# Layer 0 of a two-layer block: each part of the features written to DRAM once and repeated by the loads, sums of the weights taken from SBUF, reciprocals stored once

## The chip, the cores and the metric

The kernel runs on one core of a Trainium2 chip. The metric is the device time of one execution in microseconds; before the change its median is 2718.08 us of three runs (2716.01 to 2725.01).

The core's engines run side by side, each through its own instructions in order: TensorE (PE in the profile, with its weight loads as PEld), VectorE (DVE), ScalarE (ACT), GpSimd (POOL) and SyncE (SP), which here does nothing but issue DMAs. Sixteen DMA engines move the data. SBUF is the on-chip memory of 128 partitions, PSUM the accumulators that TensorE writes.

## The reference

Two layers of gated cross-attention and mixture-of-experts work on 64 sequences of 128 positions and 128 channels; 77 context rows belong to each sequence. The change concerns the attention of layer 0 alone:

```python
def _feature_map(x, fm_w, fm_b):
    z = jnp.einsum('nshd,ed->nshe', x, fm_w) + fm_b
    return jnp.concatenate([jnp.exp(z), jnp.exp(-z)], axis=-1)
...
v, k, q = (_feature_map(x, fm_w, fm_b) for x in (v, k, q))
scores = jnp.einsum('nqhd,nkhd->nhqk', q, k) / jnp.sqrt(jnp.float32(EMBED))
attn = jax.nn.softmax(scores, axis=-1)
out = jnp.einsum('nhql,nlhd->nqhd', attn, v)
out = out.reshape(N, S, HEADS * EXP_DIM)
return out @ fc_w.T + fc_b
```

There are 16 heads of 8 channels; the features of a head are 16, the eight exponentials of z and the eight of -z. Queries come from the normalized x, keys and values from the context. After it come layer 0's experts (eight, of width 336, with a learned number of them for each row), layer 1's attention with relative positions, and layer 1's experts (eight of width 256, the best two).

## The kernel before

**Units.** Layer 0 works on 32 units of two sequences (`NU = 2`, so 256 query columns `UT` and 154 context columns `UK`). The loop in `run` (L1086) goes through them as a pipeline: in step k it weaves together `l0_project` of unit k-3, `l0_weighted` of k-2, `l0_maxima` of k-1, `l0_features` of k, in every other step `l0_route`, and a "tape" of pieces of the experts of earlier groups. `PLAN` gives each stream a stretch of the step and a priority; the instructions are then laid out for each engine by a planner that works with its own estimates of durations. What each engine runs is fixed by that order.

**Features** (`l0_features`, L290). x and the context are loaded (L296, L298), normalized, transposed (L304, L306) and multiplied by a block matrix (L311) into the PSUM tile `pz`: rows are (feature, head), 128 of them, columns are the 256 query and the 154 context positions. ACT takes the exponential of z and of -z, queries and context apart (L315, L316), into the tile `f` (called `feat` in the profile). TensorE transposes the context's part for the values (L327).

Scores are wanted in nearly full precision from bfloat16 products. So `split3` (L132) cuts the features into three bfloat16 parts that add up to them, in the tile `f3`, 128 partitions by 3 parts by 820 columns: DVE copies part 0 (L135), POOL subtracts it (L136), DVE copies part 1 (L137), POOL subtracts again into part 2 (L138). A product is then the sum of six pairs of parts. The six pairs lie on the contraction axis: `qst` has 96 partitions, six times 16 features, of 16 heads by 256 columns, with query parts 0,0,0,1,1,2; `kst` the same of 16 heads by 154 columns, with key parts 0,1,2,0,1,0. In `f3` the partitions are (feature, head), in `qst` and `kst` they are (pair, feature) with the heads along the row, so the data go through DRAM: `stack_out` (L140) writes the arrays `dq` and `dk` with each part as often as it is needed (six stores), and four loads (L340, L342) bring them back, those of the features of z to partitions 0 to 47 and those of -z to 48 to 95. A row of a load is one head's 256 or 154 columns, 512 or 308 bytes. All these DMAs go out on SP.

**Scores.** `l0_maxima` (L346) multiplies `qst[:96]` and `kst[:96]` (L355) for the largest score of each row and head; its negative, split in three, is loaded into `qst`'s partitions 96 to 98 (L371) beside rows of ones in `kst`. `l0_weighted` (L373) multiplies again with all 99 partitions (L396), so that the maximum is taken off within the product, takes the exponential (L399) and multiplies by the values (L385). The values have a column of ones, so the product's row 16 of each group of 32 partitions is the sum of the weights. ACT copies the result to the tile `av` (L388): 128 partitions (four groups j of 32 rows), 4 heads, 2 sequences, 128 queries.

**Normalization** (`normalize`, L428, called from L409). `av` is stored to the DRAM array `od` (L408). From there `den`, the sums, is loaded to 32 partitions (L435), and `o`, the 16 feature rows of each head, to 128 (L439, two loads). DVE takes the reciprocal (L440); it is stored 16 times over to `dr` (L442), loaded as `rr` in the layout of `o` (L445), and POOL multiplies (L446). `l0_project` (L411) multiplies `o` by the output weights (L420).

Of the kernel before, what the change touches and what calls it, by code (L numbers as in the profile page):

```python
# [10 lines left out]
F32 = mybir.dt.float32  # L11
F32R = mybir.dt.float32r
BF16 = mybir.dt.bfloat16
AF = mybir.ActivationFunctionType
# [6 lines left out]
KL = 77  # L21
NH = 16
# [6 lines left out]
NU = 2  # L29
UT = NU * S  # L30
UK = NU * KL
# [10 lines left out]
def weave(tc, streams, marks=None):  # L42
# [30 lines left out]
    out=(0,0.2,2000,0),  # L73
# [31 lines left out]
class Net:  # L105
# [26 lines left out]
    def split3(self, f, out3):  # L132
# [3 lines left out]
        nc.gpsimd.tensor_tensor(f, f, out3[:, 0], ALU.subtract)  # L136
        nc.vector.tensor_copy(out3[:, 1], f)  # L137
        nc.gpsimd.tensor_tensor(out3[:, 2], f, out3[:, 1], ALU.subtract)  # L138

    def stack_out(self, dq, dk, f3, nq):  # L140

        nc = self.nc
        for n, c, p in ((0, 3, 0), (3, 2, 1), (5, 1, 2)):
            nc.sync.dma_start(out=dq[n : n + c].rearrange("i p t -> p i t"),
                              in_=f3[:, p, :nq].unsqueeze(1).to_broadcast([128, c, nq]))
            nc.sync.dma_start(out=dk[n : n + c].rearrange("i p t -> p i t"), in_=f3[:, :c, nq:])

    def stack_q(self, dq, f3, nq):
        for n, c, p in ((0, 3, 0), (3, 2, 1), (5, 1, 2)):
# [140 lines left out]
    def l0_features(self, u, st):  # L290
        nc, i, tc = self.nc, self.i, self.tc
        a, pm, dp = self.ap, self.pmisc, self.dp
        b0 = u * NU
        kst, (vf, va) = self.kst[u % 3], self.va[u % 3]
        xg = self.f0.tile([128, NU, 128], F32, tag="xg", bufs=4, name="xg")
        nc.sync.dma_start(out=xg, in_=i["x"][b0 : b0 + NU].rearrange("b p d -> p b d"))  # L296
        cg = a.tile([KL, NU, 128], F32, tag="cg", bufs=2, name="cg")
        nc.sync.dma_start(out=cg, in_=i["ctx_1024"][b0 : b0 + NU].rearrange("b p d -> p b d"))  # L298
        xn = self.layernorm(xg, NU, a, "a")
        nc.gpsimd.tensor_tensor(xg, xg, self.fcb.unsqueeze(1).to_broadcast([128, NU, 128]), ALU.add)  # L300
        NT = UT + UK
        pt = pm.tile([128, 512], F32, tag="misc", name="pt")
        for b in range(NU):
            nc.tensor.transpose(pt[:, b * S : (b + 1) * S], xn[:, b, :], self.ident)  # L304
        for b in range(NU):
            nc.tensor.transpose(pt[:, UT + b * KL : UT + (b + 1) * KL], cg[:, b, :], self.ident[:KL, :KL])  # L306
        xT = a.tile([128, NT], F32, tag="xT", bufs=1, name="xT")
        nc.scalar.copy(xT, pt[:, :NT])
        yield
        pz = pm.tile([128, 512], F32, tag="misc", name="pz")  # L310
        nc.tensor.matmul(pz[:, :NT], lhsT=self.fmW, rhs=xT, start=True, stop=True)  # L311

        f = a.tile([128, 2 * NT], F32, tag="feat", bufs=1, name="feat")
        for n, sign in ((0, 1.0), (1, -1.0)):
            nc.scalar.activation(f[:, n * UT : (n + 1) * UT], pz[:, :UT], AF.Exp, bias=self.fmb[:, n : n + 1], scale=sign)  # L315
            nc.scalar.activation(f[:, 2 * UT + n * UK : 2 * UT + (n + 1) * UK], pz[:, UT:NT], AF.Exp,  # L316
                                 bias=self.fmb[:, n : n + 1], scale=sign)
        yield
        if u < 3:
            with tc.issue_after(self.ln_last.ins):  # L320
                nc.vector.memset(kst[96:99], 1.0)
            nc.gpsimd.memset(va[:, :, :, 16:17], 1.0)

        for b in range(NU):
            pv = pm.tile([128, 512], F32, tag="misc", name="pv")
            for s in range(2):
                nc.tensor.transpose(pv[:KL, s * 128 : (s + 1) * 128],  # L327
                                    f[:, 2 * UT + s * UK + b * KL : 2 * UT + s * UK + (b + 1) * KL], self.ident)
            nc.scalar.copy(va[:, b, :, 0:16],
                                  pv[:KL, :256].rearrange("p (c h) -> p h c", h=NH))  # L330
        f3 = a.tile([128, 3, 2 * NT], BF16, tag="f3", bufs=1, name="f3")
        yield
        self.split3(f, f3)
        yield
        dq = dp.tile([6, 128, 2 * UT], BF16, tag="dq", name="dq")
        dk = dp.tile([6, 128, 2 * UK], BF16, tag="dk", name="dk")
        self.stack_out(dq, dk, f3, 2 * UT)
        qst = a.tile([99, NH, UT], BF16, tag="qst", bufs=3, name="qst")
        for n in range(2):
            nc.sync.dma_start(out=qst[48 * n : 48 * n + 48],  # L340
                              in_=dq[:, :, n * UT : (n + 1) * UT].rearrange("i (e h) t -> (i e) h t", h=NH))
            self.last_dma = nc.sync.dma_start(out=kst[48 * n : 48 * n + 48],  # L342
                              in_=dk[:, :, n * UK : (n + 1) * UK].rearrange("i (e h) t -> (i e) h t", h=NH))
        st[u] = dict(xg=xg, qst=qst, kst=kst, va=vf, spare=[Spare(self.pGU, self.gub)] * 4 if u < 2 else [])

    def l0_maxima(self, s):  # L346
# [26 lines left out]
    def l0_weighted(self, s):  # L373

        nc, a = self.nc, self.ap
        ps_t, qst, kst, va = self.pST, s["qst"], s["kst"], s["va"]
        av = a.tile([128, 4, NU, 128], F32, tag="av", bufs=1, name="av")
# [13 lines left out]
        for b in range(NU):  # L391
            for hg in range(4):
                st = next(banks).tile([128, 4, 128], F32, tag="ST", name="ST")
                for j in range(4):
                    h = 4 * j + hg
                    nc.tensor.matmul(st[:KL, j, :], lhsT=kst[:, h, b * KL : (b + 1) * KL],  # L396
                                     rhs=qst[:, h, b * S : (b + 1) * S], start=True, stop=True)
                p = a.tile([KL, 4, 128], F32, tag="P", bufs=3, name="P")
# [7 lines left out]
        T = NU * S  # L406
        od = self.dp.tile([4, 32, 4, T], F32, tag="od16", name="od")
        nc.sync.dma_start(out=od.rearrange("j r g t -> (j r) g t"), in_=av.rearrange("p g b q -> p g (b q)"))  # L408
        s["o"] = self.normalize(od, 16, NU)  # L409

    def l0_project(self, u, s, x1s):  # L411
        nc, pm = self.nc, self.pmisc
# [12 lines left out]
            x1s[u // 2] = self.x1n  # L425
        yield

    def normalize(self, od, nd, n):  # L428


        nc, a, dp = self.nc, self.ap, self.dp
        nch = nd * NH // 128
        T = n * S
        den = a.tile([NH * n, 128], F32, tag="den", bufs=1, name="den")
        nc.sync.dma_start(out=den, in_=od[:, nd].rearrange("j g (b q) -> j (g b) q", b=n))  # L435
        o = self.f0.tile([128, nch, T], F32, tag="o", bufs=2, name="o")
        ny = 4 // nch
        for y in range(ny):
            nc.sync.dma_start(out=o[y::ny], in_=od[:, :nd, y * nch : (y + 1) * nch].rearrange("j d c t -> d j (c t)"))  # L439
        nc.vector.reciprocal(den, den)  # L440
        dr = dp.tile([nd, NH * n, 128], F32, tag=f"dr{nd}_{n}", name="dr")
        nc.sync.dma_start(out=dr.rearrange("d p q -> p d q"),  # L442
                          in_=den.unsqueeze(1).to_broadcast([NH * n, nd, 128]))
        rr = a.tile([128, nch, T], F32, tag="rr", bufs=1, name="rr")
        nc.sync.dma_start(out=rr, in_=dr.rearrange("d (x c b) q -> (d x) c (b q)", c=nch, b=n))  # L445
        nc.gpsimd.tensor_tensor(o, o, rr, ALU.mult)  # L446
        return o

# [814 lines left out]
```

## Time and profile before

The profile is one execution taken by the hardware profiler.

| | |
|---|---|
| time of the profiled execution | 2721.63 us |
| its span, first to last instruction | 2719.9 us |
| mean granted TensorE clock | 0.94 |
| PE busy | 2409.3 us (89%) |
| DVE busy | 1996.1 us (73%) |
| ACT busy | 1563.2 us (57%) |
| POOL busy | 1551.5 us (57%) |
| DMA packets, data | 468652, 282.16 MB, 104 GB/s |
| L342 `kst` loads | 64, first issue 25.3 us, last 1263.4 us |
| stretch 420 to 1260 us: PE busy | 770.96 us of 840 |

In the profile "L355" is line 355 of the kernel; "out<-in" are the tiles written and read. A wait belongs to the instruction that waited and names what ended it. "The chain" is the work that ended last, followed back from the end: at each step to what released it, or to the instruction before it on its engine. The granted clock is the share of its full speed at which TensorE was let run. Layer 0 covers about the first half of the span, layer 1 the second. In the list of transfers, `dq<-f` and `dk<-f` are the six stores, `qst<-dq` and `kst<-dk` the loads.

### The profile page before, as it was taken

How to read it: one execution, taken by the hardware profiler on the slowest of the kernel's cores; microseconds unless marked ns; L12 is line 12 of the kernel's file. 1: busy time of each engine (PE TensorE's matmuls, PEld its weight loads, DVE VectorE, ACT ScalarE, POOL GpSimd, SP SyncE). 2: the span in 40 equal slices, each digit the busy share in tenths (PEclk: the TensorE clock that was granted, in tenths of full speed). 3: DMA queues.
4: the chain of work that ended last, by engine and by line, in shares of the span. 5: the costliest groups of instructions: out<-in, count | busy, mean ns of one | idle time of the engine just before them, and what ended most of it. 6: DMA issues, size and time to landing. Idle time of an engine off the chain costs nothing.

```text
span 2719.9 us, 60927 instructions
## 1 busy us (share of the span) xinstructions
PE 2409.3 (89%) x23574; PEld 1655.9 (61%) x23574; DVE 1996.1 (73%) x4165; ACT 1563.2 (57%) x3030; POOL 1551.5 (57%) x1508
## 2 busy tenths in 40 slices
PE   3688989999989899999897798998999998999996
PEld 2466666666666666666565565666666666666654
DVE  3368788888888888887785466776677676766676
ACT  2455555656555556555454356666666666666665
POOL 4455465555565555554566355665666666656556
PEclk9989899999999999999997689999999999999999
DMA  6744355354454443453235655545555655655400
GB/s 140 172 107 93 78 114 117 93 107 104 83 122 106 94 111 91 100 120 73 57 80 130 137 115 112 119 110 107 107 112 109 121 127 116 126 111 109 95 16 8
DMA packets 468652, 282.16 MB, mean 104 GB/s; under 512 B 231030, under 2 KB 446974, under 8 KB 468267
## 3 DMA queue, kind: packets, MB, share of 16 engines
q1 hardware_dynamic: 440715, 237.89, 43.4%
q10 hardware_dynamic: 27648, 40.38, 4.3%
q8 instruction: 185, 3.03, 0.5%
q14 instruction: 104, 0.85, 0.1%
HBM read 143.00 MB, written 134.40 MB: 102 GB/s over the span
## 4 chain that ended last, share of the span: by engine, by line
PE 49%; DMA 16%; DVE 13%; POOL 9%; issue 7%; ACT 3%; SPq 3%; POOLq 0%; ACTq 0%; DVEq 0%
DMA kst<-dk 5%; PE ST L837 4%; PE py L165 3%; PE py L166 3%; PE py L167 3%; PE AV L845 3%; DMA dk<-f 2%; PE AV L385 2%; POOL hl L1001 2%; PE S L780 2%; PE pu L165 2%; PE pg L165 2%; PE pz L165 2%; PE S L885 2%; POOL f L138 2%
## 5 line engine op out<-in xcount | busy, mean ns | idle before, releaser
L524 POOL TENSOR_TENSOR hl<-t,hh 128x512 fp32r<-128x512 f32 x336 | 441.8, 1317 | 352.3 <-ACT hh L523 348.2
L1001 POOL TENSOR_TENSOR hl<-t,hh 128x512 fp32r<-128x512 f32 x256 | 347.0, 1371 | 148.0 <-ACT hh L1000 145.3
L829 POOL TENSOR_TENSOR sc<-sc,mx 128x308 f32<-128x308 f32 x256 | 190.3, 747 | 229.4 <-DVE mx L828 94.8
L523 ACT CAST hh<-t 128x512 fp32r<-128x512 f32 x336 | 207.2, 617 | 162.5 <-PE py L167 68.8
L516 ACT ACTIVATE t<-pg 128x512 f32<-128x512 f32 x336 | 200.9, 598 | 158.3 <-PE pg L167 114.2
L517 DVE SCALAR_TENSOR_TENSOR t<-t,pg 128x512 f32<-128x512 f32 x336 | 227.7, 678 | 74.6 <-ACT t L516 74.0
L838 ACT ACTIVATE rel<-ST 77x512 f32<-77x512 f32 x256 | 157.7, 616 | 170.4 <-PE ST L837 166.7
L518 DVE TENSOR_TENSOR t<-t,pu 128x512 f32<-128x512 f32 x336 | 227.3, 677 | 15.1 <-PE pu L167 6.7
L623 DVE TENSOR_TENSOR ys<-sb,py 128x512 f32<-128x512 f32 x224 | 152.0, 679 | 79.2 <-PE py L167 78.3
L827 DVE TENSOR_TENSOR sc<-S,rq 128x308 f32<-128x308 f32 x256 | 120.2, 472 | 120.6 <-PE ST L837 50.3
L614 ACT COPY sb<-pb 128x512 f32<-128x512 f32 x256 | 150.5, 588 | 97.4 <-PE pb L609 94.2
L837 PE MATMUL ST<-ident,sc 128*128 128x128 f32 (+1 forms) x1024 | 173.9, 296 | 35.1 <-POOL sc L829 33.0
L1000 ACT CAST hh<-t 128x512 fp32r<-128x512 f32 x256 | 155.5, 622 | 83.6 <-PE py L167 75.0
L993 ACT ACTIVATE t<-pz 128x512 f32<-128x512 f32 x256 | 151.9, 600 | 69.9 <-POOL hl L1001 64.1
L399 ACT ACTIVATE P<-ST 77x512 f32<-77x512 f32 x256 | 151.0, 591 | 57.9 <-PE ST L396 55.1
L165 PE MATMUL py<-hh,wd_h 128*128 128x512 f32 x336 | 156.9, 467 | 18.5 <-ACT sb L614 11.9
L165 PE MATMUL pg<-xh,wg_h 128*128 128x512 f32 x336 | 159.9, 476 | 11.5 <-DVE t L518 10.5
L358 DVE TENSOR_REDUCE mx<-S 128x5 f32<-128x385 f32 (+1 forms) x192 | 110.4, 577 | 78.2 <-PE S L355 76.6
L837 PEld LDWEIGHTS ST<-ident,sc 128*128 128x128 f32 (+1 forms) x1024 | 126.4, 152 | 66.6 <-POOL sc L829 42.0
L165 PE MATMUL pu<-xh,wu_h 128*128 128x512 f32 x336 | 159.9, 476 | 5.0 <-DVE t L517 4.5
L166 PE MATMUL py<-hl,wd_h 128*128 128x512 f32 x336 | 148.6, 442 | 2.3 <-POOL hl L524 2.3
L995 DVE TENSOR_TENSOR t<-t 128x512 f32<-128x512 f32 x128 | 106.6, 833 | 50.9 <-ACT t L993 50.8
(247 smaller groups left out, 6627.4 us busy)
## 6 DMA issues: line engine op xcount, KB each, us to landing
rq<-ra SPq DMA_DIRECT2D x256, 154.0 KB
qst<-dq SPq DMA_DIRECT2D x96, 384.0 KB
ra<-sg ACTq DMA_DIRECT2D x128, 192.5 KB
kst<-dk SPq DMA_DIRECT2D x96, 231.0 KB
dq<-f SPq DMA_DIRECT2D x47, 384.0 KB
od<-av SPq DMA_DIRECT2D x32, 512.0 KB
ra<-sg ACTq DMA_DIRECT2D x64, 231.0 KB
dq<-f SPq DMA_DIRECT2D x47, 256.0 KB
```

The source lines that it names most:

```text
L165: nc.tensor.matmul(ps, lhsT=wh, rhs=xh, start=start, stop=False)
L166: nc.tensor.matmul(ps, lhsT=wh, rhs=xl, start=False, stop=False)
L516: nc.scalar.activation(t, pg, AF.Tanh, scale=0.5)
L517: nc.vector.scalar_tensor_tensor(t, t, 1.0, pg, ALU.add, ALU.mult)
L518: nc.vector.tensor_tensor(t, t, pu, ALU.mult)
L523: nc.scalar.copy(hh, t)
L524: nc.gpsimd.tensor_tensor(hl, t, hh.bitcast(F32), ALU.subtract)
L829: nc.gpsimd.tensor_tensor(sc, sc, m.unsqueeze(2).to_broadcast([128, 4, KL]), ALU.subtract)
L837: nc.tensor.transpose(st[:r, j, :], sc.rearrange("q j k -> q (j k)")[:, j * KL : j * KL + r], self.ident)
L838: nc.scalar.activation(relg[:KL, hg, b], st[:KL].rearrange("k j (q e) -> k j q e", e=2), AF.Exp, scale=1.0 / math.sqrt(HD))
L1000: nc.scalar.copy(hh, t)
L1001: nc.gpsimd.tensor_tensor(hl, t, hh.bitcast(F32), ALU.subtract)
```

## The change

Five things change, all in layer 0:

1. The exponentials write `f` with query and context columns side by side for each sign, so one ACT instruction of 410 columns takes the place of two (L315, L316). `f` now has the order (sign, query columns, context columns).
2. `stack_out` is gone. Each part is stored once, queries and context together: parts 0 and 1 to `d01`, part 2 to `d2`, two stores on SP.
3. Six loads take the place of four. A load that needs a part or a pair of parts several times has a source whose outermost dimension repeats it (`to_broadcast`): `qst` partitions 0 to 47 are part 0 three times, `kst` 16 to 79 are parts 0 and 1 twice, `qst` 48 to 79 are part 1 twice; `kst` 80 to 95 are part 0, `qst` 80 to 95 and `kst` 0 to 15 are part 2. The pairs are then in another order (query parts 0,0,0,1,1,2 against key parts 2,0,1,0,1,0), and all 16 features of a pair lie together. The loads that need part 0 and 1 alone come first.
4. `den` is loaded straight from `av` in SBUF, not from `od`.
5. `dr` holds each reciprocal once; the load of `rr` repeats it 16 times.

```diff
-    def stack_out(self, dq, dk, f3, nq):
-        nc = self.nc
-        for n, c, p in ((0, 3, 0), (3, 2, 1), (5, 1, 2)):
-            nc.sync.dma_start(out=dq[n : n + c].rearrange("i p t -> p i t"),
-                              in_=f3[:, p, :nq].unsqueeze(1).to_broadcast([128, c, nq]))
-            nc.sync.dma_start(out=dk[n : n + c].rearrange("i p t -> p i t"), in_=f3[:, :c, nq:])
...
         for n, sign in ((0, 1.0), (1, -1.0)):
-            nc.scalar.activation(f[:, n * UT : (n + 1) * UT], pz[:, :UT], AF.Exp, bias=self.fmb[:, n : n + 1], scale=sign)
-            nc.scalar.activation(f[:, 2 * UT + n * UK : 2 * UT + (n + 1) * UK], pz[:, UT:NT], AF.Exp,
-                                 bias=self.fmb[:, n : n + 1], scale=sign)
+            nc.scalar.activation(f[:, n * NT : (n + 1) * NT], pz[:, :NT], AF.Exp, bias=self.fmb[:, n : n + 1], scale=sign)
...
-        dq = dp.tile([6, 128, 2 * UT], BF16, tag="dq", name="dq")
-        dk = dp.tile([6, 128, 2 * UK], BF16, tag="dk", name="dk")
-        self.stack_out(dq, dk, f3, 2 * UT)
+        d01 = dp.tile([2, 256, NT], BF16, tag="d01", name="d01")
+        d2 = dp.tile([1, 256, NT], BF16, tag="d2", name="d2")
+        for d, p0, p1 in ((d01, 0, 2), (d2, 2, 3)):
+            nc.sync.dma_start(out=d.rearrange("i (n p) t -> p (i n) t", n=2),
+                              in_=f3[:, p0:p1].rearrange("p i (n t) -> p (i n) t", n=2))
         qst = a.tile([99, NH, UT], BF16, tag="qst", bufs=3, name="qst")
-        for n in range(2):
-            nc.sync.dma_start(out=qst[48 * n : 48 * n + 48],
-                              in_=dq[:, :, n * UT : (n + 1) * UT].rearrange("i (e h) t -> (i e) h t", h=NH))
-            self.last_dma = nc.sync.dma_start(out=kst[48 * n : 48 * n + 48],
-                              in_=dk[:, :, n * UK : (n + 1) * UK].rearrange("i (e h) t -> (i e) h t", h=NH))
+        q, k = slice(0, UT), slice(UT, NT)
+        for to, row, n, src in ((qst, 0, 3, d01[:1, :, q]), (kst, 16, 2, d01[:, :, k]), (qst, 48, 2, d01[1:, :, q]),
+                                (kst, 80, 1, d01[:1, :, k]), (qst, 80, 1, d2[:, :, q]), (kst, 0, 1, d2[:, :, k])):
+            src = src.rearrange("i p t -> (i p) t")
+            rows = n * src.shape[0] // 16
+            if n > 1:
+                src = src.unsqueeze(0).to_broadcast([n, *src.shape])
+            self.last_dma = nc.sync.dma_start(out=to[row : row + rows], in_=src)
...
-        s["o"] = self.normalize(od, 16, NU)
+        s["o"] = self.normalize(av, od, 16, NU)
...
-        nc.sync.dma_start(out=den, in_=od[:, nd].rearrange("j g (b q) -> j (g b) q", b=n))
+        nc.sync.dma_start(out=den, in_=av[nd::32].rearrange("j g b q -> j (g b) q"))
...
-        dr = dp.tile([nd, NH * n, 128], F32, tag=f"dr{nd}_{n}", name="dr")
-        nc.sync.dma_start(out=dr.rearrange("d p q -> p d q"),
-                          in_=den.unsqueeze(1).to_broadcast([NH * n, nd, 128]))
+        dr = dp.tile([NH * n, 128], F32, tag=f"dr{nd}_{n}", name="dr")
+        nc.sync.dma_start(out=dr, in_=den)
         rr = a.tile([128, nch, T], F32, tag="rr", bufs=1, name="rr")
-        nc.sync.dma_start(out=rr, in_=dr.rearrange("d (x c b) q -> (d x) c (b q)", c=nch, b=n))
+        nc.sync.dma_start(out=rr, in_=dr.rearrange("p q -> (p q)").unsqueeze(0).to_broadcast([nd, NH * n * 128]))
```

More of the change, by code (lines that the diff above doesn't have):

```diff
@@ L327, in l0_features @@
                 nc.tensor.transpose(pv[:KL, s * 128 : (s + 1) * 128],
-                                    f[:, 2 * UT + s * UK + b * KL : 2 * UT + s * UK + (b + 1) * KL], self.ident)
+                                    f[:, s * NT + UT + b * KL : s * NT + UT + (b + 1) * KL], self.ident)
             nc.scalar.copy(va[:, b, :, 0:16],
@@ L426, in l0_project, with normalize @@
         yield
-    def normalize(self, od, nd, n):
+    def normalize(self, av, od, nd, n):
         nc, a, dp = self.nc, self.ap, self.dp
```

## The prediction

> **What bounds the kernel now.** I read the page's chain first, then the chain piece by piece in the middle of layer 0, then the waits, then the DMA view in short windows. The page's chain, by engine and by line:
>
> ```profile
> PE 49%; DMA 16%; DVE 13%; POOL 9%; issue 7%; ACT 3%; SPq 3%; POOLq 0%; ACTq 0%; DVEq 0%
> DMA kst<-dk 5%; PE ST L837 4%; PE py L165 3%; PE py L166 3%; PE py L167 3%; PE AV L845 3%; DMA dk<-f 2%; PE AV L385 2%; POOL hl L1001 2%; PE S L780 2%; PE pu L165 2%; PE pg L165 2%; PE pz L165 2%; PE S L885 2%; POOL f L138 2%
> ```
>
> The largest single piece is the load of the stacked key parts, and the stores before it are there too; both occur only in layer 0, the first half of the span. The chain in order of time (start, duration, what) over two units:
>
> ```profile
> 871.31 1.76 POOL f L138
> ...
> 873.09 2.94 DMA dk<-f
> ...
> 879.06 8.53 DMA kst<-dk
> 887.63 0.55 PE S L355 x6
> ...
> 923.19 2.21 POOL f L138
> ...
> 927.40 3.34 DMA dk<-f
> ...
> 932.77 8.30 DMA kst<-dk
> 941.11 0.37 PE S L355 x6
> ```
>
> The reader is to see a loop: split (L138 ends at 873.07), store, load, score matmuls L355, and within the next unit's features the split again. From the end of the split to the first L355 it takes 14.6 us in the one unit (873.07 to 887.63) and 15.7 in the other (925.40 to 941.11): 15.1 on average. The rest of a unit's 42 us (20 units lie between 420 and 1260 us) is the way from L355 to the next split. TensorE is busy for 771 of those 840 us, 38.5 us a unit, so this loop and TensorE's own work are nearly level. The waits say so as well:
>
> ```profile
> PE S L355 <- DMA kst<-dk: 48.6, 19, 11.5
> ```
>
> Us in total, times, longest. A shorter loop can give back little more than this; a longer one is paid in full, for TensorE issues in order.
>
> **What a DMA's speed hangs on.** Three quiet windows, each with one transfer alone: the 32 rows of `den` (source four groups, destination 32 partitions), a `cg` load (77 partitions of two rows), and `rr` (128 rows of 2 KB):
>
> ```profile
> DMA packets 36, 0.02 MB, mean 27 GB/s; under 512 B 4, under 2 KB 36, under 8 KB 36
> q1 hardware_dynamic: 36, 0.02, 9.2%
> DMA packets 165, 0.08 MB, mean 88 GB/s; under 512 B 11, under 2 KB 165, under 8 KB 165
> DMA packets 144, 0.26 MB, mean 125 GB/s; under 512 B 16, under 2 KB 16, under 8 KB 144
> ```
>
> Beside 32, 154 and 128 data packets there are 4, 11 and 16 small ones. I read these as one closing packet for each DMA engine that took part: 4, 11 and 16 is the largest number up to 16 that divides the outermost size of both sides (4 and 32; 77 and 77; 16 and 128). The rates: `den`'s window of 0.6 us has 9.2% of 16 engines over 36 packets, 24.5 ns each for 512 B. For 308 B rows, first a quiet microsecond of layer 1, then two crowded windows of layer 0's own loads (2 us, mostly 512 B, and 1 us, mostly 308 B):
>
> ```profile
> q1 hardware_dynamic: 481, 0.14, 55.3%
> q1 hardware_dynamic: 500, 0.25, 124.5%
> q1 hardware_dynamic: 589, 0.20, 128.5%
> ```
>
> Quiet: 0.553 x 16 us over 481, 18.4 ns. Crowded, by throughput: 16 engines x 2 us over 500, 64 ns; 16 x 1 us over 589, 27 ns.
>
> **Part 1, the loads.** Now four loads of 768 rows each run on 48 partitions, a multiple of 16: 192 rows an engine. After, three loads have the copies outermost in their source: three copies onto 48 partitions (`qst`, 768 rows of 512 B), two onto 64 (`kst`, 1024 of 308 B), two onto 32 (`qst`, 512 of 512 B). By the reading above they get three, two and two engines, and if the same engines serve all three, two of them carry 256 + 512 + 256 rows. That the three share engines no row shows; on separate ones the busiest would have 512 short rows, 9.4 us (rival C). I take them as shared, since nothing in the program spreads them. The other three loads have 256 rows on 16 engines. The work of the slowest engine: 512 x 24.5 = 12.5 us, 512 x 18.4 = 9.4 us, and 48 rows of the single loads, 1.0 us: 22.9. I add 1.0 for what shares the ring (part three's store, and half the time `od`) and 2.1 for the fixed part of a transfer (`den` takes 2.27 us in the chain, eight rows of it 0.2). That makes 26.0 us from the first of these loads to the last landing. The crowded rates would give 512 x 64 + 512 x 27 = 46.6 instead of 21.9. I take the quiet ones, because two or three engines are nearest to `den`'s four; the crowded rows had all sixteen at once.
>
> [...]
>
> **Part 2, the stores.** Six stores with a wait become two. Parts one and two go out when the L137 copy ends (869.79 and 922.10 in these units) and take 2.9 us, so they have landed when L138 ends. Part three's store is issued then, 0.5 us, and the first load follows it on SP: 0.5 us after the split. The loads of part three wait for its 2.9 us behind that, covered by the long ones. So L355 starts 26.5 us after the split, against 15.1: **+11.4 us a unit**.
>
> **Part 3, ACT.** Two 256-column (475 ns) and two 154-column (398 ns) exponentials become two of 410: 0.755 ns a column makes 591 each, **-0.6 us** a unit, on the way to the split.
>
> **Part 4, weights' sums.** `den` no longer waits for `od` (2.6 us) and `dr` stores 16 KB instead of 256. I cost this at nothing: its end, L446's product, is needed by L420 only at 907.41, 20 us after L355, and POOL waited for `rr` 18.1 us in the whole run. That is the most it can give; it is no part of the sum.
>
> **What is late next.** SP issues in order, and I take it that an engine serves in order too, so all that is issued behind the burst arrives after it: `n3` into `qst` (L396 waits), `od`, then `o` (SP itself waits for `od`, and holds the next `xg`), and `rr`. With 2.3 + 0.9 + 2.9 + 2.7 us from `den` to `rr` behind the burst, POOL's L446 comes up to 5 us late in the units where `od` goes out beside the loads, half of them: between 0 and 2.5 a unit, I take **+0.8**, as POOL is 57% busy. TensorE's order is laid out by a planner; it may put up to 3 us of other matmuls behind L355 instead of before it, as the shorter store path would suggest: 0 to 3, I take **+1.5**. And a long wait leaves TensorE slow:
>
> ```profile
> 887.60:894.40 6.80, 6.52 (x23) 4.68 (x23) 5.04 (x11) 1.58 (x3) 1.28 (x1) 0.52 0.38 81
> 894.40:907.00 12.60, 12.60 (x125) 8.70 (x123) 10.77 (x22) 8.55 (x17) 7.88 (x8) 1.00 0.01 2
> ```
>
> Busy time by engine, then granted clock, DMA share, GB/s. After the wait of 873 to 887 the clock is 0.52 for 6.8 us, 3.3 us lost. Other units show half of that already; if all get the long one, about **+0.7** (0 to 1.7).
>
> **The sum.** 11.4 - 0.6 + 0.8 + 1.5 + 0.7 = 13.8 us a unit, 31 units (the first has no loop to lengthen): 428 us. The profiled execution took 2721.63 us (span 2719.9), 3.5 above the median of the runs: 3150 against its own time, 3146 against the median. I say **3150 us**.
>
> **Rivals.** *B, crowded rates on few engines*: 24.7 us a unit more, 3910 us. For it: the crowded windows are these very loads. Against: 16 engines made the crowd. *C, the loads spread after all*, or run on separate engines, so that the change doesn't narrow the path: the way from split to L355 becomes about 0.5 + 10 us, the loop drops out, and the time falls by about the 48.6 us of waiting, to 2675: faster. The place is the three repeated loads. Against it stands `den`, whose destination had 32 partitions and still got four engines. It decides where the busiest engine's 22.9 us fall below 11.5 (15.1 less 0.5, 2.1 and 1.0), at about half its rows, so four engines for a doubled load. *D, few engines but hidden*: the planner puts 14 us of expert matmuls in front of L355. TensorE's 38.5 us would then rule again: 2720, or up to 2900 in part. Against: in both units L355 follows the landing at once, so nothing is left in front of it.
>
> **How the numbers follow.** The forecast A has 0.76, B 0.08, C 0.08, D 0.08. A's own bounds: all extras at zero 3050; with 2.5, 3 and 1.7 and a tenth more for the rows 3350; a quarter of the way to the crowded rates and those extras 3470. For 8 in 10 I take 2960 to 3540, which holds nearly all of A and the near ends of B and D. Faster by over 0.3% (about what a measurement of this kernel can tell from no change): C and a little of D, 0.09; within: part of D, 0.02; slower: 0.89.
>
> **What would show it.** TensorE's wait at L355 near 400 us instead of 48.6; a load of `kst` from part one and two landing 20 us or more after its issue; some 20 us in every unit with the DMA share near 2 or 3 engines of 16; TensorE at 6 to 7 tenths over the first half of a longer span; the clock at half after each wait; layer 1 unchanged. I am wrong if all six loads land within 12 us of the first issue (C), or if they last 26 us and TensorE does not wait (D).

## The result, and the profile after

The changed kernel takes 3426.89 us (median of four runs, 3420.49 to 3429.2), the kernel before 2721.55 in the same comparison: a ratio of 1.2585, with an interval of 1.2547 to 1.2624. That is 705 us more. The forecast was 3150 us with a range of 2960 to 3540.

The page's first parts, after:

```profile
span 3427.5 us, 60726 instructions
PE 2447.0 (71%) x23574; PEld 1675.9 (49%) x23574; DVE 1975.9 (58%) x4165; ACT 1558.3 (45%) x2966; POOL 1552.0 (45%) x1508
PE   1346566567567567567566589788999899999997
PEclk9868788778778778778778799789999999999998
DMA  2422212212212212212212213576555556665420
```

TensorE's work is what it was (2447 us against 2409.3), but from the 4th to the 23rd of the 40 slices it is busy only 5 to 7 tenths, with a clock of 7 to 8 tenths, and the DMA engines are 1 to 2 tenths busy: little moves, and TensorE waits for it. From the score matmuls of the last unit to the end of the span it takes 1447 us (1980.7 to 3427.5) against 1448 before (1271.7 to 2719.9). All of the loss lies in layer 0's units.

The chain that ended last, by engine and by line, and the waits (us in total, times, longest):

```profile
PE 41%; SPq 22%; DMA 12%; DVE 11%; POOL 6%; issue 5%; ACT 3%; ACTq 0%; DVEq 0%; POOLq 0%
SPq L340 16%; SPq L368 3%; PE ST L833 3%; PE py L157 3%; DMA kst<-d 3%; PE py L158 3%; DMA d<-f 3%; PE py L159 2%; PE AV L841 2%; PE AV L382 2%; PE S L776 2%; PE pu L157 2%; POOL hl L997 2%; DMA den<-av 2%; PE pg L157 2%
```

```profile
PE S L352 <- DMA kst<-d: 439.6, 28, 32.4
DVE den L437 <- DMA den<-av: 256.5, 13, 24.6
PE ST L393 <- DMA qst<-n: 234.9, 18, 19.4
```

The last two before the change, in the same order:

```profile
DVE den L440 <- DMA den<-od: 17.0, 16, 8.3
PE ST L396 <- DMA qst<-n: 28.1, 19, 2.4
```

L352 is the score matmul (L355 before), L393 that of `l0_weighted` (L396 before), and L340 the issue of the six loads. The wait before the scores went from 48.6 to 439.6 us. The loss has a second place: the maxima `n3` for L393 are issued on SP among the feature loads. In a unit, 14.7 us of TensorE's idle time lie before L352 and 8.5 before L393 (1.3 and 0.9 before the change), both between the split and the scores. New is SP's own queue: 22% of the chain against 3%. The chain in order of time shows why (start, us, what; from the first store of a unit to its first score matmul):

```profile
1044.99 5.73 DMA d<-f
1050.74 0.80 SPq L340
1051.59 7.32 SPq L340
1058.97 11.64 SPq L368
1070.65 0.65 SPq L340
1071.34 5.17 SPq L340
1076.61 0.56 SPq L340
1077.22 5.54 DMA kst<-d
1083.01 0.55 PE S L352 x6
```

The split of this unit ends at 1048.7. The chain doesn't run through the first load's transfer but through SP's instructions: L340 holds SP for 7.32 us where an issue otherwise takes 0.5 to 0.8, and the small load of `n3` (L368) behind it for 11.64. All that SP has still to issue stands behind them. In the next unit it is the loads themselves (SP's own instructions, start and us):

```profile
1105.57 0.77 SPq L340 DMA_DIRECT2D qst<-d  x1
1106.39 5.98 SPq L340 DMA_DIRECT2D kst<-d  x1
1112.42 11.95 SPq L340 DMA_DIRECT2D qst<-d  x1
1124.42 5.89 SPq L340 DMA_DIRECT2D kst<-d  x1
```

The rows of the DMA records say how fast each load goes. Of 512 B rows some 90 a microsecond start while the triple load (three copies) runs; the double load (two copies) of `kst` settles at 114 rows of 308 B, the double load of `qst` at 74 rows of 512 B. Two windows of the DMA view, 3 us each, inside the triple load (1109.5 to 1112.5) and inside the double load of `kst` (1119.5 to 1122.5):

```profile
q1 hardware_dynamic: 263, 0.13, 23.5%
q1 hardware_dynamic: 342, 0.11, 15.4%
```

Columns: packets, MB, share of sixteen engines. The share is packet time over the time of sixteen engines; the count carries the reading here: 88 and 114 rows a microsecond.

Averaged over units 10 to 29, this is where a unit's time went:

| stretch, us a unit | before | after | more | forecast |
|---|---|---|---|---|
| end of split to first load | 4.0 | 2.1 | -1.9 | -3.5 |
| first load to first score matmul | 11.3 | 32.2 | +20.9 | +14.9 |
| first score matmul to next split | 26.1 | 30.0 | +3.9 | +2.4 |
| the unit | 41.4 | 64.35 | +23.0 | +13.8 |

The forecast column is set out here against the 15.1 us from split to scores of the prediction's own two units. 31 units of 23.0 are 713 us, where 705 were measured. TensorE is idle 24.6 us of a unit, against 3.4.

### The profile page after: what moved, and what is told of

Read it like the earlier page. It is cut to its first block, busy times and chain, and to the rows that moved or that the text cites. A ratio compares the mean times of both kernels' runs of the same rounds, so it can differ in the third digit from the quotient of the medians.

```text
span 3427.5 us, 60726 instructions
## 1 busy us (share of the span) xinstructions
PE 2447.0 (71%) x23574; PEld 1675.9 (49%) x23574; DVE 1975.9 (58%) x4165; ACT 1558.3 (45%) x2966; POOL 1552.0 (45%) x1508
## 4 chain that ended last, share of the span: by engine, by line
PE 41%; SPq 22%; DMA 12%; DVE 11%; POOL 6%; issue 5%; ACT 3%; ACTq 0%; DVEq 0%; POOLq 0%
SPq L340 16%; SPq L368 3%; PE ST L833 3%; PE py L157 3%; DMA kst<-d 3%; PE py L158 3%; DMA d<-f 3%; PE py L159 2%; PE AV L841 2%; PE AV L382 2%; PE S L776 2%; PE pu L157 2%; POOL hl L997 2%; DMA den<-av 2%; PE pg L157 2%
## 5 line engine op out<-in xcount | busy, mean ns | idle before, releaser
L352 PE MATMUL S<-kst,qst 96*128 96x77 bf16 x1024 | 77.9, 219 | 539.3 <-DMA kst<-d 439.6
L352 PEld LDWEIGHTS <-qst 96*128 96x128 bf16 x1024 | 55.8, 109 | 582.5 <-issue 382.5
L396 ACT ACTIVATE P<-ST 77x512 f32<-77x512 f32 x256 | 150.7, 590 | 394.9 <-PE ST L393 391.8
L355 DVE TENSOR_REDUCE mx<-S 128x5 f32<-128x385 f32 (+1 forms) x192 | 110.6, 578 | 328.0 <-PE S L352 326.5
L393 PE MATMUL ST<-qst,kst 99*77 99x128 bf16 x1024 | 111.0, 238 | 236.0 <-DMA qst<-n 234.9
L393 PEld LDWEIGHTS <-kst 99*77 99x77 bf16 x1024 | 93.4, 129 | 280.6 <-issue 203.5
L157 PE MATMUL pu<-xh,wu_h 128*128 128x512 f32 x336 | 169.9, 506 | 12.4 <-DVE t L513 11.8
L437 DVE RECIPROCAL den<-den 32x128 f32<-32x128 f32 x32 | 30.0, 936 | 256.5 <-DMA den<-av 256.5
```

Source lines behind the costliest of these rows:

```text
L157: nc.tensor.matmul(ps, lhsT=wh, rhs=xh, start=start, stop=False)
```

## The experiments

Times are medians, each ratio against the kernel before run beside it. Where a kernel is the changed one with an edit, the diff stands against the changed kernel, otherwise against the kernel before; that of the last experiment stands against `norm_only`.

**Undo the repeats.** The stores and the normalization stay those of the changed kernel; every copy has a load of its own, ten loads in all.

```diff
-            rows = n * src.shape[0] // 16
-            if n > 1:
-                src = src.unsqueeze(0).to_broadcast([n, *src.shape])
-            self.last_dma = nc.sync.dma_start(out=to[row : row + rows], in_=src)
+            c = src.shape[0] // 16
+            for j in range(n):
+                self.last_dma = nc.sync.dma_start(out=to[row + j * c : row + (j + 1) * c], in_=src)
```

> The repeating loads become single loads, one for each copy (ten loads of 256 or 512 rows, none with a copy count outermost); all else is as after the change. Theory (few engines: the outermost count of 3 or 2 sets how many DMA engines a load gets, and two of them carry 1024 rows): every load gets 16 engines, some 192 rows an engine as before the change, split to first score matmul falls from 34 us to 11 to 15, the unit from 64 to 40 to 42 us, the time to 2660 to 2740 us. Rival (repeated reads: rows of DRAM that are read two or three times are slow whoever reads them): the copies still read the same rows, the time stays above 3200 us. Rival (held engines: VectorE held by the reciprocal that waits for den is what costs): den still follows on the same queue; the time stays above 3100 us unless the loads themselves get short.

Measured: 2758.64 us, ratio 1.013 (1.0081 to 1.0179). The same bytes in the same rows: 668 of the 705 us are gone, so they belong to the repeats alone. The wait before the scores:

```profile
PE S L351 <- DMA kst<-d: 24.7, 6, 14.1
```

The pages also tell on how many engines the loads ran, by their small packets. First the changed kernel, then this one:

```profile
DMA packets 426379, 254.12 MB, mean 74 GB/s; under 512 B 228694, under 2 KB 404702, under 8 KB 425995
DMA packets 429739, 254.13 MB, mean 92 GB/s; under 512 B 232054, under 2 KB 408062, under 8 KB 429355
```

The prediction read the small packets beside a transfer as one closing packet for each engine that took part. The records of the changed kernel bear that out for the unit whose loads start at 1105.57: packets of 4 B begin at 1113.9 and twice at 1117.1, three in all, for the triple load, and at 1122.9 and 1126.3 for the double load of `kst`. That load's rows go at 114 a microsecond ahead of its first one (114 packets in 1121 to 1122) and at 57 between the two (85 in 1123 to 1124.5). This kernel has 3360 packets under 512 B more, 105 a unit. Ten loads on sixteen engines close with 160 packets; six loads on 3, 2, 2 and three times 16 engines close with 55, which is 105 fewer.

Even so the kernel isn't faster than before, and my price of 2660 to 2740 for this case missed; more on that below.

**One repeat, or the other.** `one_triple` keeps only the load with three copies (the diff); `doubles_only`, with 2 in place of 3 in its condition, keeps only the two with two.

```diff
-            rows = n * src.shape[0] // 16
-            if n > 1:
-                src = src.unsqueeze(0).to_broadcast([n, *src.shape])
-            self.last_dma = nc.sync.dma_start(out=to[row : row + rows], in_=src)
+            c = src.shape[0] // 16
+            if n == 3:
+                self.last_dma = nc.sync.dma_start(out=to[row : row + n * c],
+                                                  in_=src.unsqueeze(0).to_broadcast([n, *src.shape]))
+                continue
+            for j in range(n):
+                self.last_dma = nc.sync.dma_start(out=to[row + j * c : row + (j + 1) * c], in_=src)
```

> Only the first query load keeps its three copies in one DMA, the other repeating loads are split as in the run before. Theory (few engines): three engines carry 256 rows of 512 B, 6.3 us at the quiet rate and 10 us at the 39 ns a row that the slower two of them showed in the profile of after, and 144 rows of the other loads on top, 3 to 6 us; split to score matmul 18 to 22 us instead of 34, the time 2800 to 2950 us. Rival (repeated reads): little changes against after, above 3200 us. Rival (held engines): above 3100 us.

> The complement of the run with one triple: the triple query load is split into three single loads, the two loads that repeat a pair (key parts 0 and 1, query part 1) stay as they are after the change. Theory (few engines, the busiest one's rows set the time): two engines carry 512 rows of 308 B at 17.5 ns and 256 of 512 B at 27 ns (rates of these loads in the profile of after), 15.9 us, and some 6 us of other rows; first load to score matmul 23 to 26 us, against 32 in after, 22 with the triple alone and 16 without; the unit 55 to 58 us, the time 3130 to 3250 us. If the number of repeating loads counted and not the rows, it would lie nearer to after, 3250 to 3350 us.

Measured: 3104.26 us, ratio 1.1397 (1.135 to 1.1443), and 3242.44 us, ratio 1.1914 (1.1873 to 1.1954). The doubles' time is within what was expected, though first load to scores takes 28.3 us where 23 to 26 were; the single triple costs 150 us more than its upper end. I had thought of the other loads as running beside it on the free engines. SP's instructions of a unit show that the next one holds SP for most of the triple's run:

```profile
1090.95 0.80 SPq L339 DMA_DIRECT2D qst<-d  x1
1091.79 7.23 SPq L343 DMA_DIRECT2D kst<-d  x2
1099.06 3.38 SPq L343 DMA_DIRECT2D qst<-d  x2
```

So the other loads go out late even where they have free engines: the way from first load to scores is 22.3 us here, 28.3 with the doubles and 32.2 with all three. The closing packets (4 bytes each) are 45 and 60 a unit fewer than in `split_all`: three engines once in place of sixteen three times, and two engines twice in place of sixteen four times.

**Is it the zero step?** Part 0 is stored three times, 257 rows apart, and the triple load reads them with a real stride, three blocks outermost.

```diff
+        d0 = dp.tile([3, 257, NT], BF16, tag="d0", name="d0")
+        for j in range(3):
+            nc.sync.dma_start(out=d0[j, :256].rearrange("(n p) t -> p n t", n=2),
+                              in_=f3[:, 0].rearrange("p (n t) -> p n t", n=2))
...
+            if n == 3:
+                self.last_dma = nc.sync.dma_start(out=to[row : row + 48], in_=d0[:, :256, q])
+                continue
```

> The change as it is, but part 0 is also stored three times, to rows of DRAM 257 apart, and the first query load reads these three copies (outermost count 3, a real step) instead of one copy three times (step zero). Three small stores more. Theory (few engines, by the count): the load still runs on three engines, at 10 us as in after: 3380 to 3480 us. Variant (the count sets the engines, but reading the same bytes from three engines makes them slow, 39 instead of 26 ns a row): the load takes 6.7 us, the time falls by up to 100 us, 3310 to 3370 us. Rival (the zero step, not the count, narrows the transfer): the load gets 16 engines, 8 us less a unit, 3150 to 3200 us.

Measured: 3535.59 us, ratio 1.2983 (1.2931 to 1.3036). The triple load still runs at some 92 rows a microsecond (89 in the changed kernel), and the closing packets say three engines:

```profile
DMA packets 452492, 274.29 MB, mean 78 GB/s; under 512 B 230230, under 2 KB 430814, under 8 KB 452107
```

That is 1824 under 512 B fewer than in `split_all`, 57 a unit, so 103 closing packets: the 55 of the changed kernel and 48 of the three stores more. So neither the zero step nor reading the same bytes three times makes the load narrow; the outermost size of 3 is left. The time lies 56 us above the upper end of what was expected: SP's order changed with the three stores, and `kst`'s double load goes out 13 us behind the triple instead of 1. The time thus says little here, the packets decide.

**Are the engines behind it held as well?** The load of `den` goes on ACT's queue.

```diff
-        nc.sync.dma_start(out=den, in_=av[nd::32].rearrange("j g b q -> j (g b) q"))
+        nc.scalar.dma_start(out=den, in_=av[nd::32].rearrange("j g b q -> j (g b) q"))
```

> The change as it is, but the load of den (the sums) goes out on ScalarE's queue instead of SyncE's, so it no longer waits behind the repeating loads there. Theory (few engines): the 256 us that VectorE waits for den run beside TensorE's wait for the loads; the time stays at 3380 to 3430 us, the loop's 34 us from split to score matmul stay. Rival (held engines): VectorE's 13 waits of up to 24 us are paid, the time falls by 100 to 250 us, to 3180 to 3330 us.

Measured: 3462.71 us, ratio 1.2714 (1.2664 to 1.2765). DVE's wait for `den` falls from 256.5 to 44.7 us, and the kernel is 36 us slower than the changed one all the same, above both ranges. That wait lay beside the loads; what the 36 us are stays open.

**Where the triple lands.** The triple load's copies go to partitions 48, 64 and 80 instead of 0, 16 and 32; the double of `qst` goes to 16 and 32.

```diff
-        for to, row, n, src in ((qst, 0, 3, d01[:1, :, q]), (kst, 16, 2, d01[:, :, k]), (qst, 48, 2, d01[1:, :, q]),
-                                (kst, 80, 1, d01[:1, :, k]), (qst, 80, 1, d2[:, :, q]), (kst, 0, 1, d2[:, :, k])):
+        for to, row, n, src in ((qst, 48, 3, d01[:1, :, q]), (kst, 16, 2, d01[:, :, k]), (qst, 16, 2, d01[1:, :, q]),
+                                (kst, 0, 1, d01[:1, :, k]), (qst, 0, 1, d2[:, :, q]), (kst, 80, 1, d2[:, :, k])):
```

> The change with the six pairs in another order of partitions, the same loads otherwise: the triple query load goes to partitions 48 to 95 (its three engines at 48, 64 and 80) instead of 0 to 47 (0, 16 and 32); the double query load to 16 to 47. [...] Rival (three engines on one load are slow wherever they write): 3400 to 3450 us.

Measured: 3419.19 us, ratio 1.2553 (1.2517 to 1.2588): unchanged in time, as the rival has it, but not in the transfers, where its reason fails. Windows of 3 us inside the triple load and inside the first half of the double load of `kst` (1104.5 to 1107.5 and 1109.8 to 1112.8):

```profile
q1 hardware_dynamic: 336, 0.17, 22.6%
q1 hardware_dynamic: 249, 0.08, 15.7%
```

The triple goes from 88 to 112 rows a microsecond; over units 12 to 29 its rows run from 1.7 to 9.3 us behind the issue, against 1.7 to 12.2. But `kst`'s double now has 83 rows a microsecond in its first half, and ends at 20.5 us against 21.4. In the kernel with the doubles alone the double of `kst`, on the same partitions 16 to 47 and 48 to 79, has 76 rows a microsecond first (306 in 4 us) and 114 later (342 of 308 B in 3 us). In the changed kernel its rows begin at 57 and go on at 114: the triple's closing packets come at 1113.9 and 1117.1, so its two engines start about 3 us apart, and the slow first half is missing. So the triple's pace changed with its partitions, and the double's with how far apart its engines started; why, no run shows. That the triple's gain and the double's loss cancel is read from the rates and wasn't tested by itself.

**The repeats inside, on sixteen engines.** All of the change, but row r, copy n lands on partition 3r+n (2r+n for the doubles), and the other operand is laid out to match. The outermost size is then 16. Two more things differ. The two stores hold the queries and the keys, three parts each, so neither leaves before the split ends. And a packet of these loads carries all 16 heads of a partition, 8192 or 4928 B, so a unit has 192 packets where it had 3072.

```diff
-        for d, p0, p1 in ((d01, 0, 2), (d2, 2, 3)):
...
+        g3 = f3.rearrange("p i (n t) -> p (i n) t", n=2)
+        for d, sl in ((dq, slice(0, UT)), (dk, slice(UT, NT))):
+            nc.sync.dma_start(out=d.rearrange("i (n p) t -> p (i n) t", n=2), in_=g3[:, :, sl])
...
+        for to, row, n, src in ((qst, 0, 3, dq[:1]), (kst, 0, 3, dk), (qst, 48, 2, dq[1:2]),
+                                (kst, 48, 2, dk[:2]), (qst, 80, 1, dq[2:]), (kst, 80, 1, dk[:1])):
+            src = src.rearrange("i (r h) t -> r i (h t)", h=NH).to_broadcast([16, n, NH * src.shape[2]])
+            self.last_dma = nc.sync.dma_start(out=to[row : row + 16 * n], in_=src)
```

> All of the change, but the copies of a row stand inside it: the destination takes row r, copy n on partition 3r+n, so the outermost size of each repeated load is 16 rows and not 3 or 2 copies (the rows of the other operand are laid out to match; six loads, two stores, every load a run of 16 heads per partition). Theory 1, the outermost size sets the engines and a zero step inside costs nothing: all 16 engines carry each load, no issue holds SP for microseconds, the way from the split to the first score matmul is 10 to 16 us, and the time is 2680 to 2790 us, near the kernel before (the compiled order has 37 expert matmuls a unit between the scores and the next features, against 34 before, which would take 1 us a unit of any gain away). Theory 2, a repeated source is narrow wherever the repeat stands: the wait at the scores stays above 200 us and the time is above 3000 us.

Measured: 2746.81 us, ratio 1.009 (1.006 to 1.0121). The wait before the scores is back to the size of before:

```profile
PE S L348 <- DMA kst<-dk: 63.9, 24, 10.3
```

Two of the loads, those of `qst`, still repeat rows with a zero step, and 680 of the 705 us are gone. The closing packets are 64 a unit fewer than in `split_all`: 96, six loads on sixteen engines each. So here the place of the repeat decided on the engines, not the repeat. How much of the time the longer packets give this run doesn't part; `split_all` gets 668 us with the short ones. An issue takes SP 0.6 us at the median. The way from split to scores is 14.2 us, 1.1 shorter than before. The way from scores to split is 29.5 us, some 3.5 longer, and that makes it slower than the kernel before. Some of it can be named: TensorE's granted clock in this stretch is 0.91 against 0.97 before, which is some 1.5 us, and 37 expert matmuls stand before the next features where 34 stood, 1.3 us at 0.43 each.

**The normalization alone.** `norm_only` is the kernel before with parts 4 and 5 of the change. `sums_only` has part 4 alone (the first two edits of the diff), `recip_only` part 5 alone (the last two). `split_oldnorm` is `split_all` with the old normalization.

```diff
-        s["o"] = self.normalize(od, 16, NU)
+        s["o"] = self.normalize(av, od, 16, NU)
...
-        nc.sync.dma_start(out=den, in_=od[:, nd].rearrange("j g (b q) -> j (g b) q", b=n))
+        nc.sync.dma_start(out=den, in_=av[nd::32].rearrange("j g b q -> j (g b) q"))
...
-        dr = dp.tile([nd, NH * n, 128], F32, tag=f"dr{nd}_{n}", name="dr")
-        nc.sync.dma_start(out=dr.rearrange("d p q -> p d q"),
-                          in_=den.unsqueeze(1).to_broadcast([NH * n, nd, 128]))
+        dr = dp.tile([NH * n, 128], F32, tag=f"dr{nd}_{n}", name="dr")
+        nc.sync.dma_start(out=dr, in_=den)
...
-        nc.sync.dma_start(out=rr, in_=dr.rearrange("d (x c b) q -> (d x) c (b q)", c=nch, b=n))
+        nc.sync.dma_start(out=rr, in_=dr.rearrange("p q -> (p q)").unsqueeze(0).to_broadcast([nd, NH * n * 128]))
```

> The kernel before with parts 4 and 5 of the change alone: den from av in SBUF, each reciprocal stored once and repeated 16 times by the load of rr. Prediction's reading (off the path, at most the 18 us that GpSimd waited for rr): 2695 to 2722 us. Rival (it is this part that makes the split version 1.3% slower than before, since SyncE's order changes or den is late): 2730 to 2765 us.

> The version with ten single loads, with the normalization as it was before the change (den from od, 16 copies of the reciprocals stored). If the loss of 1.3% of the split version comes from the normalization: 2700 to 2725 us. If it comes from the ten loads, the stores or the order that the planner makes of them: 2740 to 2780 us. Theory of the loop (loads on all engines cannot make the unit longer, the split version shows no wait of TensorE for them): the first is the likelier one by a little.

> The kernel before with one edit: the weights' sums are read from SBUF; the reciprocals are stored sixteen times as before. The stores and the loads of the features are those of before. Of the 64 us by which both edits of the normalization slow the kernel: theory 1, it is the order of TensorE's instructions. In the compiled order the expert matmuls between the features and the scores, which cover the loads, go from 62 a unit to 58.5 with this edit alone, against 60.3 with both and 61.8 with the other edit alone; so this one costs most, 2750 to 2800 us. Theory 2, it is the read of reciprocals that were stored once (POOL's wait for them went from 18 to 55 us): this one costs nothing, 2715 to 2730 us.

> The kernel before with the other edit: the reciprocals are stored once and the load repeats them; the weights' sums still come from DRAM. Theory 1 (the order, whose cover stays at 61.8 expert matmuls a unit against 62): 2710 to 2745 us. Theory 2 (the read of reciprocals stored once is late, and what waits for the product follows): 2760 to 2790 us, with POOL's wait for the reciprocals again near 55 us.

Measured: 2782.02 us, ratio 1.0203 (1.0178 to 1.0229); 2799.08, ratio 1.0277 (1.0249 to 1.0305); 2767.57, ratio 1.0158 (1.012 to 1.0195); 2786.37, ratio 1.024 (1.0203 to 1.0277). Each half slows the kernel before, and both together cost no more than the second alone: they don't add. `norm_only` and `split_oldnorm` lie above every range that was expected for them, by 17 and 19 us. With the loads split, the new normalization is even the faster one (1.013 against 1.0277). Either edit raises POOL's wait for the reciprocals from 18.1 us to 61.5 and 65.7, so the part for `recip_only` of the theory of the late read held, and its part for `sums_only` fell; for the theory of the order it was the other way round. From `norm_only`:

```profile
PE S L355 <- DMA kst<-dk: 90.2, 26, 11.0
POOL o L445 <- DMA rr<-dr: 55.0, 23, 8.2
DVE x L422 <- PE pf L420: 35.8, 14, 13.8
```

Before, these three were 48.6, 18.1 and 6.8. The reciprocals should come sooner, but the planner also places the product earlier in POOL's queue: it starts 6.0 us after the split of the unit two further on, against 13.0 before (8.8 and 8.9 with one half).

**Take that wait away.** `norm_only`, with the product multiplying by a constant in SBUF; the reciprocals are still loaded, and the sums aren't divided out. The last two lines tell the planner that the product comes after the load, without a wait on the chip.

```diff
-        nc.sync.dma_start(out=rr, in_=dr.rearrange("p q -> (p q)").unsqueeze(0).to_broadcast([nd, NH * n * 128]))
-        nc.gpsimd.tensor_tensor(o, o, rr, ALU.mult)
+        ld = nc.sync.dma_start(out=rr, in_=dr.rearrange("p q -> (p q)").unsqueeze(0).to_broadcast([nd, NH * n * 128]))
+        t = nc.gpsimd.tensor_tensor(o, o, self.tg[:, 0:1].unsqueeze(2).to_broadcast([128, nch, T]), ALU.mult)
+        self.tc.add_manual_dep(t.ins, ld.ins.name, mybir.DependencyInfo(
+            mybir.DependencyClass.NoSync, mybir.DependencyReason.DATA), reason="order")
```

> The kernel before with both edits of the normalization (norm_only), and the product on POOL multiplies by a constant gate in SBUF instead of by the reciprocals: the reciprocals are loaded as before and nothing reads them, so the sums are not divided out. In the compiled order the product stands where it stood, and the expert matmuls between the scores and the next features, and between these and the next scores, are 72.5 and 119.5 a pair of units against 70.8 and 120.6. Theory 1, the product stands ahead of its data: POOL waits there (3.1 us a pair of units against 0.3 in the kernel before), DVE behind it, and DVE's idle time between scores and split goes from 1.3 to 6.9 us a pair. Without the wait the time is 2715 to 2745 us, and DVE's idle time there is under 3.5 us a pair. Theory 2, it is the order of TensorE's instructions, whatever POOL waits for: 2765 to 2800 us, with POOL's wait for the reciprocals gone.

Measured: 2743.53 us, ratio 1.0083 (1.0053 to 1.0113), at the upper end of the first theory's range and outside the second's. About 33 of the 55 us go with the wait. The figures for DVE in this expectation were mis-taken, for I had counted its semaphore instructions as work. By the busy times of the windows DVE is idle between scores and split for 6.6 us a pair of units before, 12.6 in `norm_only` and 11.3 here. So DVE did not come back, and that step of the theory falls; TensorE's idle time over the whole pair did in part (6.8, 10.6 and 8.3 us).

What is left, some 23 us here, 24 in `rows_outer` and 35 in `split_all`, stays open. The order of TensorE's instructions differs in every one of these kernels. The stretch from scores to split is longer than before here and in `rows_outer`; in `split_all` it is shorter (23.5 us against 26.1) and the way from split to scores longer (19.1 against 15.3). No run held the order fixed, so the order as their cause is only argued. None of the kernels beats the one before; the nearest are `no_rr_wait`, which leaves work out, and `rows_outer`.

## Why the prediction was right, and where it was not

- **The mechanism, part 1.** Right. The three repeated loads run on as many engines as they have copies, share these engines, and set the way from split to scores. `split_all` and `rows_outer` take back 668 and 680 of the 705 us with the same bytes, and the closing packets give 3, 2 and 2 engines. The prediction took it as an assumption that the loads share them. The records don't name the engine, but the rates fit: `kst`'s rows begin at 57 a microsecond, one engine's pace, while 512 B rows go on at some 50, and reach 114 when these end.
- **The size of part 1.** Too small: 26.0 us from first issue to scores, measured 32.2. The term that was mis-sized is the triple load, 256 x 24.5 = 6.3 us on the slowest engine. Its rows start over 10.5 us (1.7 to 12.2). In the rates (some 90 a microsecond for 7 us, then some 53) one engine keeps 26 ns a row and two go at 39. The others came out close: 512 rows of `kst` at 17.5 ns, 9.0 us against 9.4; 256 of the second `qst` at 27 ns, 6.9 against 6.3. Start, single loads and landing take the remaining 5.8 us (32.2 less 10.5, 9.0 and 6.9), against 4.1 in the sum. That the range held the truth is in part luck: its upper end was priced by crowded rates and late extras, and what used the room were two engines at 39 ns a row in the triple load, a later first load and a longer start and landing.
- **Part 2, "0.5 us after the split".** Measured 2.1. The step that failed is the store of parts one and two "take 2.9 us, so they have landed when L138 ends". The chain has 5.73 us for it in the one unit and 4.26 in the next, so it lands about 2 us after the split.
- **Part 3.** Two exponentials of 410 columns take 1.2 us (599 ns each) instead of 1.75 (477 and 396): the -0.6 us is right.
- **Part 4 and 5, "I cost this at nothing".** This failed as a step. The 18.1 us of POOL's wait were taken as the most that could change, downward; that the planner may move the product ahead of its data was not considered. Alone the two parts cost 55 us on the kernel before; 33 of them go with POOL's wait, the rest stays open. What it does inside the changed kernel no run separates; with the loads split it gained.
- **What is late next.** The stretch from scores to split grew by 3.9 us against +2.4, 0.6 of it gained by part 3. The planner's share: between scores and features stand 14 and 68 expert matmuls in the two kinds of unit, where 8 and 60 stood. The slow clock costs 2 to 3 us in this stretch of every unit, against 0 and 2 before. At 0.43 us a matmul the seven more are 3.0 us, and the clock 1.8 more: both had the direction predicted and came to their upper bounds (3 and 1.7). The late `n3` was foreseen, but its 8.5 us a unit lie between split and scores, beside the wait for the loads.
- **SP held by an issue.** Not in the prediction. It had `n3`, `od` and the rest late behind the burst, on the assumption that an engine serves in order; in fact SP often cannot even issue them in time (11.64 us in the issue of `n3` above).
- **The rivals.** Crowded rates (3910) did not come: two or three engines ran at 27 ns a row of 512 B, or 39 on two of the triple's three, and not at 64. The spread loads (C) were tried by `split_all` and `rows_outer`: the waits fall as C says, but the time comes to 2747 to 2759, not 2675. C's price left out that the planner lays out TensorE's order anew; that this is the difference is argued, not shown. Hidden loads (D) did not come: from split to scores TensorE is idle over 20 us in every unit from the third on.
- **What was to show it.** The wait near 400 us (439.6), landings 20 us behind the issue, a DMA share of 2 or 3 engines, TensorE at 5 to 7 tenths, a slow clock (0.64 on average in the 6.8 us after a unit's first score matmul, where half was named) and an unchanged layer 1 all came.

The errors add up: 1.6 + 6.0 + 1.5 us a unit are 9.1, and 31 units of it 282 us, where measured and predicted time differ by 277.

## What to carry to other kernels

A load that repeated its source ran here on all sixteen engines when the repeat stood inside, with sixteen outermost (96 closing packets a unit for six loads), and on two or three when the repeat came first (55): before writing it, look at the outermost size of both sides, and if the copies must come first, issue one load for each. Ask of a narrow load (one on few engines) also what its queue has to issue next, since the issuing engine stood still with it here, for 5 to 12 us. And in a kernel whose order a planner writes, a shorter side path is not free: price it by where the planner will then put the consumer, not only by the wait it had.

## What the runs showed of the hardware that was not expected

- **An issue that holds its engine.** SP's instruction for a load that stands behind a narrow one takes 5 to 12 us (5.98, 11.95, 5.89) instead of 0.5 to 0.8, and it need not be narrow itself: the third of these is a single load of 256 rows. In the changed kernel 70 of the 192 load issues (L340) take over 5 us, 23 of them single loads, the longest 12.1; none takes 2 us of the 192 in `rows_outer` and the 320 in `split_all`, where the closing packets give sixteen engines a load.
- **The pace of a row on a lone engine.** 27 ns for 512 B (74 rows a microsecond on the two engines of the double `qst`) and 17.5 ns for 308 B (57 on one, 114 on two, of the double `kst`). They are near the two rows of the quiet windows that the prediction took (24.5 and 18.4).
- **A pace that changed with where the copies land.** With its copies on 0, 16 and 32 the triple load had 88 rows of 512 B a microsecond, 39 ns a row on two of its engines; on 48, 64 and 80 it had 112, 27 ns a row on three. The double load of `kst`, on 16 to 47 and 48 to 79, had 76 rows of 308 B a microsecond first and 114 later in `doubles_only`, and 83 in its first half in `triple_high`. What makes these differences no run shows.
